# A two-step recurrence with its two normalisations apart, and its second set of weights at the other end of memory

## The chip, the cores and the metric

One core of a Trainium2 chip runs the whole program. The core has five engines, each with a queue of its own that it works through in order: TensorE (PE in the profile, its weight loads PEld), VectorE (DVE), ScalarE (ACT), GpSimd (POOL) and SyncE (SP), which here only starts DMAs. The metric is the device time of one execution in microseconds (us).

## The reference, cut to what matters

The input x has 2 sequences of 2048 tokens with 256 features, all float32. Six blocks add to it in turn, each on a layernorm of x:

```python
x = x + 0.5 * moe(layernorm(x))         # 6 experts, 2 per token, and a shared one
x = x + attention0(layernorm(x))        # 16 heads
x = x + 0.5 * moe(layernorm(x))         # the same weights
x = x + 0.5 * recurrence(layernorm(x))
x = x + attention1(layernorm(x))        # causal, rotary, relative positions
x = x + 0.5 * recurrence(layernorm(x))  # the same weights

def recurrence(x):      # the scan runs over the 2 sequences, so it has 2 steps
    c = in_c
    for xt in x:
        f = sigmoid(xt @ wf.T + c @ uf.T + bf)
        i = sigmoid(xt @ wi.T + c @ ui.T + bi)
        g = tanh(xt @ wc.T + c @ uc.T + bc)
        c = f * c + i * g
    return tanh(x @ wo.T + c @ uo.T + bo)
```

At the first step c is `in_c` for every token, so `in_c @ u.T + b` is a vector that is computed once.

## The kernel before, in words

x stays on the chip as 32 chunks of 128 tokens. Four chunks make a block of 512 tokens; blocks 0 to 3 are the first sequence (the recurrence's step 0), blocks 4 to 7 the second (step 1). Instructions are issued on each engine in the order in which the program is written; nothing reorders them.

A layernorm of a block is `stats` (L97 and L98 on VectorE for each chunk, then `root`, L102 and L104 on GpSimd), `normal` (L115, four instructions on VectorE, in some places on GpSimd), and `turn` (L125: eight TensorE transposes into two PSUM banks, copied out by ScalarE at L126). `Norm` keeps what is done in dictionaries, so that a block that was normalised or turned ahead is passed over. All PSUM use goes through eight banks, called `s`; normalised and turned blocks share eight slots, called `b`.

The mixture of experts works in two halves of 16 chunks. It scatters the tokens to memory sorted by expert, runs 74 tiles a half, and then adds the results back: `combine(h, c)` gathers two rows per token (L436, two indirect DMAs issued by GpSimd into a ring of ten `yg` tiles) and adds them with two L441 on VectorE. The second half's 16 combines can only come after the last expert tile; `rest(n)` issues the next n of them, followed by `last(c)`, which in the second mixture normalises a block of the next layer when its four chunks are complete. The shared expert's last two blocks (`up`, `mul`, `down`; evictions L349) run in the same place. Eight of the 16 combines stand there, and the other eight in the next layer.

The first attention is a list of jobs by step. In steps 0 to 8 only the largest scores are formed: a product (L756) and a reduction on VectorE (L760) for each of eight units a step, in two halves. Just ahead of step 0, GpSimd clears two small tiles (L556) and adds the output bias to four blocks (L588). In each half of steps 0 to 3, a combine of the rest follows the reductions. From step 9 the exponentials and weighted sums (L770, L775, L782) run beside them.

The recurrence holds the gates of a block as features by tokens. `gate(cb, step, m)` computes half m (128 features) of the three gates of block cb of a step: at step 0 six float32 products, at step 1 twelve, since the state is multiplied too (L146, two TensorE instructions to a product); then three activations on ScalarE (L896) and the new state on VectorE (L901 to L908). `first_bias` (L861 and L867) makes the three vectors of the first step; L861 is 24 small TensorE instructions. A loop over cb, four rounds, keeps step 0 a block ahead of step 1, and normalises and turns two blocks further on; `outputs` (L917 to L944) forms the result of a block pair one round late. In the first recurrence, `normals` and `turns` also normalise two blocks for the second attention in rounds 2 and 3, and the gates of step 0 are followed by `rest(2)`. In the second, blocks 0 and 4 are normalised and turned already in the tail of the second attention.

Memory is taken from pools that stack up from the left end or from the right end. A load into a place that earlier tiles held waits until those tiles have had their last reader. SP issues loads in order, so one that waits holds up those behind it. In the second recurrence the pool `wr` with the 13 weights (17 KB in each partition) lies at the right end, where the second attention's weights (`w1`, 9 KB) were; at the left end lay that attention's `mneg` tiles, its three `band` tiles and its values, and above them `part`, which collects the weighted sums. At the end of an attention group L658 transposes `part`, L672 its divided form, and L681 applies the output weights.

Of the kernel before, what the change touches and what calls it, by code (L numbers as in the profile page):

```python
# [27 lines left out]
CPB = TB // P  # L28
SB = S // TB
# [13 lines left out]
def macaron_kernel(ctx: ExitStack, tc: tile.TileContext, t: dict, out: bass.AP):  # L43
    nc = tc.nc
# [28 lines left out]
    def bank():  # L73
        return psum.tile([P, TB], F32, name="s")
# [7 lines left out]
    def pool(stack, name, bufs=1, side=None):  # L82
        return stack.enter_context(
            tc.tile_pool(name=name, bufs=bufs, side=side, reuse_waits="tile")
        )
# [72 lines left out]
    HB = NTB // 2  # L158
# [8 lines left out]
    def moe(w, ws, gate_w, gate_b, rev, tri, iota, z, behind, last, gathered):  # L167
# [3 lines left out]
        with ExitStack() as s:  # L171
# [333 lines left out]
            def rest(n):  # L505
                for _ in range(n):
                    c = next(chunks, None)
                    if c is not None:
                        combine(1, c)
                        last(c)  # L510
# [5 lines left out]
            down(6)  # L516
            rest(1)
            down(7)
            rest(4)
            if gathered is None:  # L520
                rest(HC)
            xnT.clear()
# [184 lines left out]
    def attention0(norm, tail, rest, wq, wk_, wv, wo, bff):  # L707
# [7 lines left out]
        with ExitStack() as s:  # L715
# [106 lines left out]
            for step in range(min(jobs), max(jobs) + 1):  # L822
                todo = jobs.get(step, [])
                for n in range(2):
                    z.begin(2 * step + n)
                    te, tm = (step - 9) // PER, step // PER
                    ke, um = ((step - 9) % PER) * 2 + n, (step % PER) * 2 + n
                    exps = 0 <= te < NG
                    last_j = 1 if exps else 3
                    for j in range(J):  # L830
                        if exps:
                            exponential(te, ke, j)
                        if 0 <= tm < NG:
                            largest(tm, um, (j + 2) % J if exps else j)
                    for fn, args in todo[n * (len(todo) + 1) // 2 :][: (len(todo) + 1 - n) // 2]:
                        fn(*args)
                    if step in range(4):
                        rest(1)
                    unit = 2 * (step - 9) + n - 1
                    if 0 <= unit < NG * NKB:  # L840
                        weighted(unit // NKB, unit % NKB)
# [3 lines left out]
    def recurrence(w, norm, store, rest, normals, turns):  # L845
# [3 lines left out]
        with ExitStack() as s:  # L849
# [18 lines left out]
                        bias0[n], pb[:, ds(2 * k, 2)], w[f"b{n}"], ALU.add  # L868
                    )

            def normal(cb):
                for step in range(2):
                    if step * SB + cb not in norm.xn:
                        norm.stats(step * SB + cb)
                        norm.normal(step * SB + cb, nc.vector)

            def turn(cb):
                for step in range(2):
                    if step * SB + cb not in norm.xnT:
                        norm.turn(step * SB + cb)  # L880
                    norm.xn.pop(step * SB + cb)

            def xnT(cb, step):
                return norm.xnT[step * SB + cb]
# [1 line left out]
            def gate(cb, step, m):  # L886

                g = {}
                for n, fn in GATES:
                    pg = bank()  # L890
                    mm2(pg, w[f"w{n}"], ts(m, P), xnT(cb, step), stop=step == 0)
                    if step == 1:
                        mm2(pg, w[f"u{n}"], ts(m, P), c1[cb], start=False)
                    bias = bias0[n] if step == 0 else w[f"b{n}"]
                    g[n] = wk.tile([P, TB], F32, name=f"g{n}")
                    nc.scalar.activation(g[n], pg, fn, bias=bias[:, m : m + 1])  # L896
                state = c1 if step == 0 else c2
                if m == 0:
                    state[cb] = wk.tile([P, 2, TB], F32, name=f"state{step}")
                c = state[cb][:, m, :]  # L900
                nc.vector.tensor_tensor(g["i"], g["i"], g["c"], ALU.mult)  # L901
                if step == 0:
                    nc.vector.scalar_tensor_tensor(
                        c, g["f"], w["in_c"][:, m : m + 1], g["i"], ALU.mult, ALU.add
                    )
                else:
                    nc.vector.tensor_tensor(c, g["f"], c1[cb][:, m, :], ALU.mult)
                    nc.vector.tensor_tensor(c, c, g["i"], ALU.add)  # L908
# [40 lines left out]
                    for half in range(CPB // 2):  # L949
                        output(cb, step, half, cu)  # L950

            normal(0)
            first_bias()
            turn(0)
            normal(1)
            for m in range(2):
                gate(0, 0, m)
                rest(2)
            turn(1)
            for cb in range(SB):  # L960
                if cb + 1 < SB:
                    for m in range(2):
                        gate(cb + 1, 0, m)
                        rest(2)
                if cb + 2 < SB:
                    normal(cb + 2)
                normals(cb)
                gate(cb, 1, 0)
                if cb + 2 < SB:
                    turn(cb + 2)  # L970
                turns(cb)
                gate(cb, 1, 1)
                if cb:
                    outputs(cb - 1)
            outputs(SB - 1)
# [436 lines left out]
    def recurrence_weights(wp):  # L1412
        return {
            n: load(wp, n)
            for n in (
                "wf", "uf", "wi", "ui", "wc", "uc", "wo", "uo", "bf", "bi", "bc", "bo", "in_c",
            )
        }

# [10 lines left out]
    with tc.manual_schedule(engines=ENGINES):  # L1430

        n0, n1, n2, n3, n4, n5 = (Norm() for _ in range(6))
        with ExitStack() as s:
            wp = pool(s, "wa0")


            ahead = Jobs()
            for b in range(SB):
                layernorm_jobs(ahead, n1, b, HC + 4 + CPB * b)

            weights = []

            def loads0():
                weights.extend(load(wp, n) for n in ("a0_q", "a0_k", "a0_v", "a0_o", "a0_b"))

            rest = run_moe(
                n0, ahead.run, nothing, loads0, clear=True, gathered=pool(s, "gathered")
            )
            tail = []
            for b in range(3):  # L1450
                tail += [(1 + 2 * b, n2.stats, b), (2 + 2 * b, n2.normal, b, nc.vector),
                         (3 + 2 * b, n2.turn, b)]
            tail.append((7, n2.stats, 3))
            attention0(n1, tail, rest, *weights)


        with ExitStack() as s:
            wr = pool(s, "wr")
            rec = {}

            def loads1():
                rec.update(recurrence_weights(wr))

            ahead = Jobs()
            for b in range(2):
                layernorm_jobs(ahead, n3, b, HC + 6 + CPB * b)

            def last(c):
                if c in (3, 7):
                    b = HB + c // CPB  # L1470
                    n3.stats(b)
                    n3.normal(b, nc.vector)

            rest = run_moe(n2, ahead.run, last, loads1, gathered=pool(s, "gathered"))
            w1 = ExitStack()
            wp = pool(w1, "w1", side="right")
            a = {n: load(wp, f"a1_{n}") for n in ("q", "k", "v", "o", "rel0_row")}
            relk, relv, rel0 = (load(wp, n) for n in ("relk", "relv", "rel0_col"))
            kbias = wp.tile([P, 2], F32, name="kbias")
            fp = pool(s, "rel")  # L1480
            relk0, relv0 = load(fp, "relk0"), load(fp, "relv0")

            def normals(cb):

                if cb == 1:


                    nc.vector.scalar_tensor_tensor(
                        kbias, rowsel[:, 0:2], rel0[:, 0:1], rowsel[:, 2:4], ALU.mult, ALU.add
                    )  # L1490
                    nc.vector.tensor_tensor(relk, relk, relk0, ALU.subtract)
                    nc.vector.tensor_tensor(relv, relv, relv0, ALU.subtract)
                if cb > 1:
                    n4.stats(cb - 2)
                    n4.normal(cb - 2, nc.vector)

            def turns(cb):
                if cb > 1:
                    n4.turn(cb - 2)
                    n4.xn.pop(cb - 2)  # L1500

            recurrence(rec, n3, False, rest, normals, turns)
        tail = []
        for i, b in enumerate((0, SB)):
            tail += [(3 + 2 * i, n5.stats, b), (4 + 2 * i, n5.normal, b, nc.vector),
                     (5 + 2 * i, n5.turn, b)]
        attention1(n4, tail, a, relk, relv, kbias, dramp, skew)
        w1.close()
        with ExitStack() as s:
            recurrence(recurrence_weights(pool(s, "wr", side="right")), n5, True, nothing, nothing, nothing)  # L1510


def _layout(i):
# [88 lines left out]
```

## Time and profile before

| | |
|---|---|
| three runs | 4068.05, 4071.13, 4072.09 us; median 4071.13 |
| the profiled execution | 4068.88 us, span in the profile 4067.0 us |
| granted TensorE clock, mean | 0.993 |
| first mixture, to the start of the first attention | about 0 to 347 us |
| first attention | to about 2050 us |
| second mixture | to about 2386 us |
| first recurrence | 2386 to 2578 us |
| second attention | to 3876 us |
| second recurrence | 3876 to 4067 us |

Times in the text are us from the start of the span. A row of the timeline gives the start, the duration, the engine, the line, the operation with what it writes and reads, and how many instructions it merges; in brackets stands how long the engine was idle before it, and what it waited for. A row of the waits gives who waited for whom, the sum in us, how often, and the longest. A row of the windows gives a stretch, its length, the busy time of PE, PEld, DVE, ACT and POOL (instructions in brackets), the clock that TensorE was granted as a share of full speed, the DMA engines' share, and GB/s.

### The profile page before, as it was taken

The numbers are of one execution on the slowest core, as the hardware profiler recorded it, in microseconds if no ns is written. First come the engines' busy times: TensorE is split into PE (matmuls) and PEld (weight loads), VectorE is DVE, ScalarE is ACT, GpSimd is POOL, SyncE is SP. The second block draws the span as 40 slices with busy tenths as digits, with TensorE's granted clock in tenths as the row PEclk, the third lists the DMA queues.
The fourth block names the chain that finished last, engine by engine and source line by source line (L and its number), as shares of the span: only waits on it lengthen the run. The fifth ranks groups of instructions, "written<-read, shape, count | busy, mean of one in ns | idle before, by whom it ended". The sixth has DMA issues, their size and how long they took to land.

```text
span 4067.0 us, 76436 instructions
## 1 busy us (share of the span) xinstructions
PE 3996.5 (98%) x28256; PEld 1930.7 (47%) x28256; DVE 2701.9 (66%) x6128; ACT 2568.8 (63%) x5227; POOL 1634.8 (40%) x1456
## 2 busy tenths in 40 slices
PE   8999999999999999999999999999999999999999
PEld 4665333333344333333356655555554455554445
DVE  6247888888866888888752444667677766677533
ACT  2333788888887888888833322366667766667832
POOL 4245333336333333333442340345635645544410
PEclk9999999999999999999999999999999999999999
DMA  7341000100000000000033420334533344442101
GB/s 256 122 128 58 1 1 1 48 1 1 1 1 1 1 1 1 1 1 1 10 110 126 129 76 0 78 82 104 111 71 74 82 81 87 91 96 49 45 22 42
DMA packets 355508, 223.18 MB, mean 55 GB/s; under 512 B 146624, under 2 KB 338496, under 8 KB 355136
## 3 DMA queue, kind: packets, MB, share of 16 engines
q1 hardware_dynamic: 276800, 176.33, 16.5%
q0 software_dynamic: 12288, 33.57, 2.6%
q10 hardware_dynamic: 66048, 8.39, 1.3%
q8 instruction: 225, 3.69, 0.4%
q14 instruction: 147, 1.20, 0.1%
HBM read 113.12 MB, written 105.12 MB: 54 GB/s over the span
## 4 chain that ended last, share of the span: by engine, by line
PE 90%; DVE 5%; POOL 1%; ACT 1%; issue 1%; DMA 0%; SPq 0%; POOLq 0%; ACTq 0%; DVEq 0%
PE s L770 13%; PE s L782 12%; PE s L756 10%; PE s L146 10%; PE s L1237 7%; PE s L1123 6%; PE s L383 6%; PE s L1208 6%; PE s L403 3%; PE s L681 2%; PE s L1222 1%; PE s L1201 1%; PE s L1218 1%; PE s L344 1%; PE s L931 1%
## 5 line engine op out<-in xcount | busy, mean ns | idle before, releaser
L542 POOL TENSOR_TENSOR part<-part 128x512 f32<-128x512 f32 (+3 forms) x800 | 962.0, 1203 | 1389.9 <-ACT part L644 1377.0
L760 DVE TENSOR_REDUCE mx<-s 128x1 f32<-128x512 f32 x2048 | 1271.0, 684 | 292.8 <-PE s L756 292.6
L775 ACT ACTIVATE pT<-s 128x512 f32<-128x512 f32 x2048 | 1063.6, 618 | 200.7 <-PE s L756 199.1
L756 PE MATMUL s<-kT,q 32*128 32x512 f32 x4096 | 1018.6, 618 | 1.9 <-DVE mx L760 1.9
L770 PE MATMUL s<-q,kT 32*128 32x512 f32 x4096 | 1013.0, 615 | 0.4 <-DVE q L639 0.4
L1229 ACT ACTIVATE pT<-s 128x512 f32<-128x512 f32 (+3 forms) x1280 | 587.8, 542 | 252.8 <-PE s L1208 102.0
L770 PEld LDWEIGHTS s<-q,kT 32*128 32x128 f32 x4096 | 417.8, 183 | 466.9 <-DVE mx L760 327.0
L644 ACT COPY part<-s 128x512 f32<-128x512 f32 (+3 forms) x864 | 508.2, 589 | 148.2 <-PE s L782 60.2
L1131 DVE TENSOR_REDUCE mx<-s 128x1 f32<-128x512 f32 (+1 forms) x768 | 473.0, 679 | 132.3 <-PE s L1123 123.9
L782 PE MATMUL s<-pT,v 128*32 128x512 f32 x4096 | 549.8, 605 | 0.6 <-ACT pT L775 0.2
L756 PEld LDWEIGHTS s<-kT,q 32*128 32x128 f32 x4096 | 406.4, 184 | 128.9 <-ACT pT L775 76.2
L1123 PE MATMUL s<-kT,q 32*128 32x512 f32 (+7 forms) x2240 | 332.1, 433 | 0.0
L1237 PE MATMUL s<-pT,v 128*32 128x512 f32 (+3 forms) x2560 | 304.7, 541 | 9.1 <-DVE mx L1131 5.0
L383 PE MATMUL s<-we,xT 128*128 x592 | 278.7, 593 | 0.2 <-ACT xT L378 0.2
L390 DVE TENSOR_TENSOR h<-sg,s 128x256 f32<-128x256 f32 x148 | 62.4, 422 | 289.5 <-ACT sg L388 289.3
L1123 PE MATMUL s<-b,q 32*128 32x512 f32 (+7 forms) x1280 | 243.0, 518 | 1.6 <-DVE v L612 1.4
L782 PEld LDWEIGHTS s<-pT,v 128*32 128x32 f32 x4096 | 82.1, 108 | 336.1 <-ACT pT L775 300.4
L1147 DVE CUSTOM_DVE_ANT_0 band<-s,band 128x160 f32<-128x160 f32 (+1 forms) x512 | 155.7, 314 | 127.2 <-PE s L1208 62.6
L542 POOL TENSOR_TENSOR band<-band,mneg 128x640 f32<-128x640 f32 x128 | 161.3, 1260 | 189.2 <-DVE mneg L1157 127.9
L1208 PE MATMUL s<-q,kT 32*128 32x512 f32 (+3 forms) x1152 | 236.3, 509 | 0.0
L436 POOL DMA_INDIRECT yg<-results,at x128 | 123.8, 967 | 235.0 <-DMA results<-y 197.6
L1208 PE MATMUL s<-q,b 32*128 32x512 f32 (+3 forms) x896 | 208.5, 568 | 0.0
(227 smaller groups left out, 5148.1 us busy)
## 6 DMA issues: line engine op xcount, KB each, us to landing
band<-skew SPq DMA_DIRECT2D x32, 1280.0 KB, 7.5
pd<-band SPq DMA_DIRECT2D x32, 1280.0 KB, 8.5
xs<-places SPq DMA_DIRECT2D x148, 128.0 KB, 2.2
results<-y SPq DMA_DIRECT2D x148, 128.0 KB, 1.7
places<-zero SPq DMA_DIRECT2D x2, 4736.0 KB, 16.4
we<-in_we SPq DMA_DIRECT2D x12, 768.0 KB, 11.6
skew<-s ACTq DMA_DIRECT2D x32, 256.0 KB, 3.0
s<-pd SPq DMA_DIRECT2D x32, 256.0 KB, 4.3
```

What stands on the lines that cost most here:

```text
L383: nc.tensor.matmul(pu, lhsT=xT[n][:, ts(kc, P)], rhs=w[:, kc, ds(val[n], 2 * D)], start=kc == 0, stop=kc == 1,)
L542: fn(*args)
L644: nc.scalar.copy(part[:, q0:], pv[:, q0:])
L756: nc.tensor.matmul(ps, lhsT=q[t][rows(j), ts(qb, P)], rhs=kT[b, g][rows(j), ts(kc, TB)], start=True, stop=True,)
L760: nc.vector.tensor_reduce(mx[t][:, qb * J + j, kc : kc + 1], ps, AX.X, ALU.max)
L770: nc.tensor.matmul(st, lhsT=kT[b, g][rows(j), ts(kb, P)], rhs=q[t][rows(j), :], start=True, stop=True,)
L775: nc.scalar.activation(z.pTs[t, kb, j], st, AF.Exp)
L782: nc.tensor.matmul(pv[rows(j), :], lhsT=v[b, g // 2][:, kb, ds(h * VW, 32)], rhs=z.pTs.pop((t, kb, j)), start=True, stop=True,)
L1123: nc.tensor.matmul(ps[:, ds(cols, n)], lhsT=lhsT, rhs=kT[b, c, g][rows(j), ds(k0, n)], start=True, stop=True,)
L1208: nc.tensor.matmul(ps[:, q0:], lhsT=k, rhs=q[t][rows(j), q0:], start=True, stop=True, skip_group_check=True,)
L1229: nc.scalar.activation(z.pTs[t, kb, j][:, q0:], st.pop((t, kb, j))[:, q0:], AF.Exp)
L1237: nc.tensor.matmul(pv[rows(j), q0:], lhsT=v[b, kb // CPB, g // 2][:, kb % CPB, ds(h * VW, 32)], rhs=z.pTs.pop((t, kb, j))[:, q0:], start=T ...
```

## The change

The combines that the mixture's own end issues become four instead of eight; in the first attention the others run in both halves of steps 0 to 5, and in the first recurrence behind six gates, two each. `last` normalises only the first block of the second half (block 4). In both recurrences `normal` and `turn` take one block at a time: step 1's blocks are normalised and turned one round later than step 0's blocks of the same number, and block 1's turn stands between the two gates of block 0. The 13 weights are loaded with the small vectors first, and the second recurrence's pool lies at the left end.

```diff
@@ end of moe
             down(7)
-            rest(4)
             if gathered is None:
                 rest(HC)
@@ attention0
-                    if step in range(4):
+                    if step in range(6):
                         rest(1)
@@ recurrence
-            def normal(cb):
-                for step in range(2):
-                    if step * SB + cb not in norm.xn:
-                        norm.stats(step * SB + cb)
-                        norm.normal(step * SB + cb, nc.vector)
-
-            def turn(cb):
-                for step in range(2):
-                    if step * SB + cb not in norm.xnT:
-                        norm.turn(step * SB + cb)
-                    norm.xn.pop(step * SB + cb)
+            def normal(cb, step):
+                if step * SB + cb not in norm.xn:
+                    norm.stats(step * SB + cb)
+                    norm.normal(step * SB + cb, nc.vector)
+
+            def turn(cb, step):
+                if step * SB + cb not in norm.xnT:
+                    norm.turn(step * SB + cb)
+                norm.xn.pop(step * SB + cb)
...
-            normal(0)
+            normal(0, 0)
             first_bias()
-            turn(0)
-            normal(1)
-            for m in range(2):
-                gate(0, 0, m)
-                rest(2)
-            turn(1)
+            turn(0, 0)
+            normal(1, 0)
+            gate(0, 0, 0)
+            rest(2)
+            turn(1, 0)
+            gate(0, 0, 1)
+            normal(0, 1)
+            rest(2)
             for cb in range(SB):
                 if cb + 1 < SB:
-                    for m in range(2):
-                        gate(cb + 1, 0, m)
-                        rest(2)
+                    gate(cb + 1, 0, 0)
+                    rest(2)
+                    if cb == 0:
+                        turn(0, 1)
+                    gate(cb + 1, 0, 1)
+                    rest(2)
                 if cb + 2 < SB:
-                    normal(cb + 2)
+                    normal(cb + 2, 0)
+                if cb + 1 < SB:
+                    normal(cb + 1, 1)
                 normals(cb)
                 gate(cb, 1, 0)
+                rest(2)
                 if cb + 2 < SB:
-                    turn(cb + 2)
+                    turn(cb + 2, 0)
+                if cb + 1 < SB:
+                    turn(cb + 1, 1)
                 turns(cb)
                 gate(cb, 1, 1)
+                rest(2)
                 if cb:
                     outputs(cb - 1)
@@ recurrence_weights
-                "wf", "uf", "wi", "ui", "wc", "uc", "wo", "uo", "bf", "bi", "bc", "bo", "in_c",
+                "bf", "bi", "bc", "in_c", "wf", "uf", "wi", "ui", "wc", "uc", "wo", "uo", "bo",
@@ second mixture
             def last(c):
-                if c in (3, 7):
-                    b = HB + c // CPB
-                    n3.stats(b)
-                    n3.normal(b, nc.vector)
+                if c == CPB - 1:
+                    n3.stats(HB)
+                    n3.normal(HB, nc.vector)
@@ second recurrence
-            recurrence(recurrence_weights(pool(s, "wr", side="right")), n5, True, nothing, nothing, nothing)
+            wr = pool(s, "wr")
+            recurrence(recurrence_weights(wr), n5, True, nothing, nothing, nothing)
```

## The prediction

> **What bounds the kernel now.** I read the engine shares and the chain of waits first, then the timelines of the three places that the change touches. TensorE carries the end; only holes in its row, and work that it does at half clock, can be won.
>
> ```profile
> PE 3996.5 (98%) x28256; PEld 1930.7 (47%) x28256; DVE 2701.9 (66%) x6128; ACT 2568.8 (63%) x5227; POOL 1634.8 (40%) x1456
> PE 90%; DVE 5%; POOL 1%; ACT 1%; issue 1%; DMA 0%; SPq 0%; POOLq 0%; ACTq 0%; DVEq 0%
> ```
>
> The first recurrence (2386 to 2578) has two holes, both before transposes of normalised blocks: 4.14 us for block 5, 3.35 us for block 6. After the first, ScalarE is late too.
>
> ```profile
> 2405.06 2.28 PE L125 MATMUL s<-ident,b 128*128 128x128 f32 x8 [4.14 <-DVE b L115]
> 2408.12 3.78 PE L146 MATMUL s<-b,wf 128*128 128x512 f32 x4 [0.78 <-ACT gf L896]
> 2436.29 2.21 PE L125 MATMUL s<-ident,b 128*128 128x128 f32 x8 [3.35 <-DVE b L115]
> ```
>
> The second recurrence begins with a wait for `in_c`, the last of 13 loads, of which the first had waited 41.2 us for L658, the last division's transposes (waits of SP, then the timeline):
>
> ```profile
> SPq L131 <- PE s L658: 41.2, 1, 41.2
> ```
>
> ```profile
> 3869.69 0.35 SPq L131 DMA_DIRECT2D wf<-in_wf  x1
> ...
> 3878.31 0.43 SPq L131 DMA_DIRECT2D in_c<-in_in_c  x1
> 3880.29 1.78 PEld L861 LDWEIGHTS s<-in_c,uf 128*128 128x128 f32 x8 [4.68 <-DMA bi<-in_bi]
> 3880.32 1.84 PE L861 MATMUL s<-in_c,uf 128*128 128x1 f32 x8 [4.31 <-DMA in_c<-in_in_c]
> ```
>
> The table of windows shows in its PEclk column (after the five busy times) what the hole leaves behind: half clock until about 3890.
>
> ```profile
> 3880.00:3886.00 6.00, 5.68 (x25) 5.62 (x26) 0.39 (x4) 0.15 (x1) 0.00 (x0) 0.51 0.01 3
> 3886.00:3890.00 4.00, 4.00 (x6) 1.51 (x5) 2.39 (x10) 1.81 (x2) 1.26 (x2) 0.50 0.00 0
> 3890.00:3894.00 4.00, 4.00 (x11) 1.75 (x10) 2.89 (x11) 1.37 (x2) 0.80 (x2) 0.96 0.00 0
> ```
>
> At the start of the first attention one combine instruction of VectorE (L441, median 485 ns) takes 9.97 us, while GpSimd does the bias additions:
>
> ```profile
> 350.82 9.97 DVE L441 SCALAR_TENSOR_TENSOR x<-yg,col,x 128x256 f32<-128x256 f32 x1
> 351.24 9.26 POOL L588 TENSOR_TENSOR x<-x,a_b 128x1024 f32<-128x1024 f32 x4
> 361.62 2.48 DVE L760 TENSOR_REDUCE mx<-s 128x1 f32<-128x512 f32 x4
> ```
>
> **The change, part by part.** No instruction or DMA is added or dropped: same gates, normalisations, transposes, gathers and loads, in another order. Units at full clock: a step-0 gate is 12 TensorE instructions, 5.15 us; a step-1 gate 24, 10.3; a turn (8 transposes) 0.86.
>
> *Four combines moved into the first attention.* Combine is two gathers on GpSimd (one per 1.25 us) and two L441 (0.92 us together). Before, VectorE reaches its first L760 at 361.62, though TensorE's first product (L756) is out at 356.34; it is VectorE-bound until about 408. Half a step is four L760 (2.39), with a combine 3.31. To the end of step 5 before: 361.62 + 8 x 3.31 + 0.3 + 4 x 2.4 = 398.0. After: it starts behind the product, at 356.7, with 12 combines: 356.7 + 12 x 3.31 = 396.4. Gain 1.6. GpSimd now meets memset and bias additions right behind the eight gathers of chunks 0 to 3, at 340.2; they end near 350.6, and chunk 4's gathers, with 2.9 us from issue to use, are there by 355, before their turn at 359.1. Here a rule speaks against the change. The Trainium skill, "SBUF — State Buffer", section "Who interferes with whom", says that a VectorE instruction with two SBUF inputs and a GpSimd instruction that reads SBUF exclude each other for whole instructions. The 9.97 us row agrees. So the additions, now at 341.1 to 350.6, would catch chunk 2's L441 (341.63 before), with four evictions (L349) behind it. By the rule VectorE resumes at 350.6 with four L441 and four L349, 4.8 us, and is done at 355.4: before 356.7, so the price is nothing. The four banks held can't stop TensorE, since four others are free for the projections that ScalarE empties. Without the rule the start is 356.7 as well. If the cover failed, the 4.8 us would cancel the gain: 1.6 us, between -3 and 2.
>
> *First recurrence.* Before, chunks 4 to 7 and block 5's normalisation stood on VectorE ahead of `first_bias`, so ScalarE got its biases at 2406. Now VectorE does the two evictions and the bias additions by 2391.3, and TensorE goes on from `first_bias` (ends 2388.95): three gates to 2404.4, block 4's turn (normalised at 2389.8) to 2405.3, a gate to 2410.45, the step-1 gate to 2420.75, block 2's turn to 2421.65. The next wait is block 5's. VectorE finishes the state of gate (1,0,1) 2.44 us after TensorE, 2412.9; two combines (2.0) to 2414.9; their gathers, the sixteenth at 2388.5 + 1.5 + 14 x 1.25 = 2407.5, have landed, because the two GpSimd roots now stand behind them. From the same rows of before (2427.04, 2435.73) block 5's normalisation starts 8.69 us later, 2423.55. The transposes start 0.56 behind it: the hole is 2.45 us, not 3.35. Queued on GpSimd behind block 5's root (2423.5) are the gathers of chunks 12 to 15; VectorE uses the last near 2441, and block 6 is first read for its statistics after gate (2,0,1), near 2450. That is cover.
> Is 2.45 us enough to lose the clock? The Trainium skill, "TensorE: Matmul & The Clock Gate", section "What's actually happening", puts both the idle and the busy window at about 3.4 us: no loss here. But the trace shows 0.50 in 3870 to 3872 after a hole of 2.18 us (and 0.29). I side with the row: 1.2 us, as after 2436 (the whole sum would be 22.3 by the rule, 21.1 by the row). The next gate's state product then starts at 2428.5, against 2440.70: 12.2 us won. Block 7's turn (0.86) still has to be done, now in round 2, and there it stands on VectorE ahead of the norm of the second attention, which ends 5.1 us later than its 2511.0. The turn ready at 2514.8 is held as in 2471.19 (loss 1.02 us by the starts of the next gate). Round 1 keeps its stall. Net 10.3; 8 to 13 with clock and gathers.
>
> *Second recurrence.* On the right the 17 KB of weights don't fit into the 9 KB that the attention's weights leave, so `wf` lies on `part`, which L658 reads at 3869. On the left they begin where the second attention's first tiles do: two `mneg` of 2 KB and bands of 10.4 KB, so they lie on `mneg` and the first two bands. Those are last read by the subtract transposes (3820) and the band transposes (L1218, last at 3843.2). The last older DMA of SP is issued at 3828.12; behind it all loads but `uo` and `bo` can start, and these two near 3843.5. Only the output stores (first at 3974.9) queue behind them. So 13 issues at 0.47 us and some 5 us of transfer leave the path. The new neighbour is `s<-pd`: it was issued first and takes 3.1 us, and its reader (L1254) runs at 3838.6, 7 us later. Its price is nothing; at most the 1.8 MB at the 362 GB/s seen in 3874 to 3876, 5 us, still inside that slack. `first_bias` then starts at 3876.0, not 3880.3: 4.3. At full clock it takes 2.6 us, as at 2386.35, not 5.1: 2.5; the first two gates 10.3 instead of 12.8: 2.5. By the clock page's 3.4 us window the half clock would have cost only about 1.7 us of these 5.0 and the gain would be 3.3 lower; the 0.50 rows last 9.8 us, and the trace decides. Block 1's turn now stands after one gate: its normalisation starts 3.7 us behind the bias additions, 3882.8, so the next gate starts at 3884.85 instead of 3884.67: loss 0.2. Gate (1,0,0) starts at 3889.95 against 3899.99: 10.0, less block 7's turn later (0.86, hidden on VectorE: ready 3 us ahead). Net 9.2, between 1 and 10.
>
> The new weight order costs nothing in the first recurrence: its loads run near 2052 to 2067, with first use at 2386.
>
> **Sum.** 1.6 + 10.3 + 9.2 = 21.1 us. The profiled run took 4068.9 (span 4067.0), 2.3 below the median of 4071.1; so 4047.8 for that run, and 4050.0 for the median.
>
> **Rivals.**
> Loads not early: some reader of the left region is later than I see, and the loads still end behind the last outputs. Small ones being first, about 1 us remains of part three: 21.1 - 8.2 = 12.9, 4058. Against it: nothing in the two `mneg` and two bands is read after 3844.
> The combines pace the first recurrence: with eight between gates, GpSimd's gather chain stays the path, as before (nearly all of 2388 to 2427). The hole ahead of block 5 then grows by up to 8 us: 4058. For it: L441 waited 0.7 us for each gather there. Against it: roots no longer split the chain.
> Slower: the 12 combines of the first attention run unprefetched, each waiting its gather's full 2.9 us in VectorE's queue ahead of the reductions, 35 us; then 4050 + 35 = 4085. It decides from 2.4 us a combine (29 us, the 21 plus 0.2%). Against it: ten `yg` buffers, and 0.3 us of such waits in that window.
>
> **Numbers.** My forecast 0.78 (4047 to 4057 by the bounds of parts one and two), loads late 0.08, gathers pace 0.08, both of these 0.03 (5 us left, 4066), slower 0.03. A measurement here can tell about 0.2%, 8 us, from no change. Faster: 0.78 + 0.08 + 0.08 = 0.94; same: 0.03. Range 4043 to 4060: it takes in the two milder rivals, and below 4047 the 4 us by which the runs shown differ.
>
> **What would show it.** Right: no wait of L861 for a DMA, clock 1.0 from 3876 on; `wf` issued near 3829; in the first recurrence no hole of 4 us near 2401 and one of 2 to 3 us ahead of block 5; L760 starting near 357. Wrong: a wait for `uo` or `in_c`, `s<-pd` landing after its reader is due, or VectorE idle for gathers between the reductions.

## The result, and the profile after

The kernel after takes 4050.03 us (median of 6 runs, 4046.7 to 4052.26), the kernel before 4069.84 (median of 6, 4067.27 to 4072.09): ratio 0.9954, 95% interval 0.9944 to 0.9964. The profiled execution took 4048.79 us, its span is 4046.9, and the granted clock was 0.995 on average (before: 0.993). The forecast was 4050.0. The lines of the changed kernel have other numbers than before by a few: L861 is L860, L760 is L759, L867 is L866, L658 is L657.

The engine shares in the page of the kernel after. TensorE is busy for 9.8 us less than before, though its instructions are the same ones: fewer of them ran at half clock, which makes 8.2 us by the clock records. The rest of the 20.1 us were holes.

```profile
PE 3986.7 (99%) x28256; PEld 1925.3 (48%) x28256; DVE 2698.4 (67%) x6128; ACT 2569.0 (63%) x5227; POOL 1634.6 (40%) x1456
```

The timeline of the first recurrence, kernel after (VectorE's bias additions, then TensorE). The biases are there at 2389.5 instead of 2406, the hole of 4.14 us is gone, and of the two holes one is left, 2.19 and 0.19 us ahead of block 5's transposes. Two rows are new: `wf` takes 3.01 us right behind the small products of L860, and 3.45 behind the hole, where such a row of four instructions takes 1.88 at full clock.

```profile
2389.34 0.14 DVE L866 TENSOR_TENSOR bias0f<-s,bf 128x2 f32<-128x2 f32 x1
2386.49 1.03 PE L860 MATMUL s<-in_c,uc 128*128 128x1 f32 x8
2387.39 3.01 PE L146 MATMUL s<-b,wf 128*128 128x512 f32 x4
2390.19 2.58 PE L146 MATMUL s<-b,wi 128*128 128x512 f32 x4
...
2424.17 0.56 PE L125 MATMUL s<-ident,b 128*128 128x128 f32 x2 [2.19 <-DVE b L115]
2424.93 1.24 PE L125 MATMUL s<-ident,b 128*128 128x128 f32 x6 [0.19 <-DVE b L115]
2425.97 3.45 PE L146 MATMUL s<-b,wf 128*128 128x512 f32 x4
```

The second recurrence, kernel after: SP's queue, TensorE, and then the table of windows (stretch, length, busy PE, PEld, DVE, ACT, POOL, clock, DMA share, GB/s). The loads are issued 47 us ahead of their use, L860 waits for nothing, and the clock is 1.00 where it was 0.51.

```profile
3818.11 1.19 SPq L131 DMA_DIRECT2D bf<-in_bf  x1
...
3833.18 0.43 SPq L131 DMA_DIRECT2D bo<-in_bo  x1
3865.18 0.95 PE L860 MATMUL s<-in_c,uf 128*128 128x1 f32 x8
3867.78 1.96 PE L146 MATMUL s<-b,wf 128*128 128x512 f32 x4
```

```profile
3864.00:3870.00 6.00, 6.00 (x36) 4.66 (x35) 2.98 (x12) 1.50 (x2) 0.00 (x0) 1.00 0.00 0
```

The start of the first attention, kernel after. GpSimd's additions come 10.4 us earlier than before and now catch a combine in the mixture's tail: of the two instructions in its row the first takes 8.85 us, to 0.3 us behind the end of the additions; the first reduction starts when TensorE's first product is there, 4.2 us earlier than before.

```profile
340.86 9.26 POOL L587 TENSOR_TENSOR x<-x,a_b 128x1024 f32<-128x1024 f32 x4
341.56 9.37 DVE L441 SCALAR_TENSOR_TENSOR x<-yg,col,x 128x256 f32<-128x256 f32 x2
357.43 0.69 DVE L759 TENSOR_REDUCE mx<-s 128x1 f32<-128x512 f32 x1 [3.18 <-PE s L755]
```

Where the time went, by stage. Each column is the difference of two starts in one profiled execution (us). "First attention's end" is the start of the last transposes of its divided outputs. The first recurrence runs from the first of the small bias products (L861, L860 after) to the last of its output products (L931, L928 after); the gap behind it ends at the first such transposes of the second attention. The last two columns count from the last start of the division's transposes (L658, L657 after): to the second recurrence's small products, and to the end. The last five kernels ran on two other chips (see the experiments).

| kernel | first attention's end | second mixture | first recurrence | gap behind it | small products behind division | end behind division |
|---|---|---|---|---|---|---|
| before | 2055.6 | 330.8 | 191.1 | 194.4 | 11.0 | 197.7 |
| after | 2055.7 | 329.1 | 183.1 | 193.2 | 6.6 | 188.3 |
| after, again | 2055.0 | 330.4 | 181.2 | 196.5 | 6.4 | 188.2 |
| old order, on the left | 2056.0 | 330.7 | 181.4 | 194.0 | 6.4 | 188.2 |
| first mixture's combines back | 2057.7 | 330.1 | 181.1 | 196.5 | 6.3 | 188.1 |
| turns late | 2055.4 | 329.1 | 176.2 | 196.8 | 6.3 | 186.0 |
| before, new order only | 2123.8 | 387.7 | 193.8 | 192.6 | 6.3 | 188.0 |
| before, split only | 2127.7 | 387.2 | 193.0 | 191.5 | 10.6 | 196.8 |
| after, combines back in both mixtures | 2124.5 | 387.4 | 193.1 | 194.4 | 6.4 | 188.1 |
| after, combines back in the second | 2121.3 | 388.2 | 193.2 | 194.4 | 6.4 | 188.2 |
| after, weights on the right | 2120.0 | 388.3 | 184.5 | 192.6 | 6.5 | 188.3 |

In the second mixture and in the gap TensorE's work is the same in all of these; among the first six rows the mixture differs by up to 1.7 us, and the gap by 3.6. That is the grain below which one profile of one kernel says nothing. The gain of the kernel after stands in the first recurrence and behind the division: 8.0 and 9.4 us in its first profile, 17.4 of the 20.1; the rest are differences of that grain. Of the 8.0, TensorE's idle time makes 5.9 (8.8 us before, 2.9 after) and time at half clock 1.7.

### The profile page after: what moved, and what is told of

It is laid out like the page before. It is cut to its first block, busy times and chain, and to the rows that moved or that the text cites. A ratio compares the mean times of both kernels' runs of the same rounds, so it can differ in the third digit from the quotient of the medians.

```text
span 4046.9 us, 76439 instructions
## 1 busy us (share of the span) xinstructions
PE 3986.7 (99%) x28256; PEld 1925.3 (48%) x28256; DVE 2698.4 (67%) x6128; ACT 2569.0 (63%) x5227; POOL 1634.6 (40%) x1456
## 4 chain that ended last, share of the span: by engine, by line
PE 90%; DVE 5%; POOL 2%; ACT 1%; issue 1%; DMA 1%; SPq 0%; DVEq 0%; ACTq 0%; POOLq 0%
PE s L769 13%; PE s L781 12%; PE s L755 10%; PE s L146 10%; PE s L1245 7%; PE s L383 6%; PE s L1131 6%; PE s L1216 6%; PE s L403 3%; PE s L680 2%; PE s L1230 1%; PE s L1209 1%; PE s L1226 1%; DVE mx L759 1%; PE s L928 1%; PE s L603 1%
## 5 line engine op out<-in xcount | busy, mean ns | idle before, releaser
L759 DVE TENSOR_REDUCE mx<-s 128x1 f32<-128x512 f32 x2048 | 1270.3, 682 | 297.6 <-PE s L755 297.1
```

The costliest lines, as they stand in the source:

```text
L759: nc.vector.tensor_reduce(mx[t][:, qb * J + j, kc : kc + 1], ps, AX.X, ALU.max)
```

## The experiments

The theory to begin with was the prediction's: the second recurrence gains because its weights lie where they can be loaded early; the first gains because the combines and block 5's layernorm left the way of the biases; the combines moved into the first attention gain little, as the profile after shows its end where it was. The rivals: the order of the loads does it, not their place; the combines in the first attention have a large share; the split of the layernorms has a gain of its own.

Eight of the twelve runs fell on two other chips, on which the kernel before takes 4196 us (medians 4196.36 and 4195.77), mostly because TensorE idles in the two mixtures there: the second takes 387 us instead of 331, with 45 us of idle TensorE instead of 3. The other four ran where before takes 4069.49, as in the comparison above (4069.84); in what follows that is the first chip. Each ratio is to runs of before on the same chip, and profiles are compared with profiles of the same group.

**The first part undone, with both mixtures touched.**

```diff
             down(7)
+            rest(4)
             if gathered is None:
...
-                    if step in range(6):
+                    if step in range(4):
```

> The kernel after, with the first part alone undone: the four combines stand in the first mixture again (rest(4) behind down(7), range(4) in the first attention). My theory by now: that part is worth nothing, because the 0.85 us by which VectorE is ahead in step 6 is eaten by a half-clock spell of TensorE that lasts longer; so the time of the kernel after, 4050, within 2 us, and the first product of the first attention that is read (the reduction of L759) at about 361.6 instead of 357.4. Rival, the prediction's sum: 1.6 us slower than after, 4051.6. Rival, the part was the whole gain: 4070.

Measured: 4188.3 us, ratio 0.998 (0.9972 to 0.9988), when the kernel with all of the change but the place of the weights has 0.9943 in the same group (below). That is far more than the few us expected, and the table says where: the first recurrence takes 193.1 us instead of 184. The edit was blunter than its text: the tail of the mixture is one function for both mixtures, and `rest(4)` came back in the second one too, ahead of the first recurrence. So the run is not a test of the first part; it showed how much hangs on the second mixture's four combines, with the reservation made below, where they come back alone.

**The weights alone, left and in the new order.**

```diff
-                "wf", "uf", "wi", "ui", "wc", "uc", "wo", "uo", "bf", "bi", "bc", "bo", "in_c",
+                "bf", "bi", "bc", "in_c", "wf", "uf", "wi", "ui", "wc", "uc", "wo", "uo", "bo",
...
-            recurrence(recurrence_weights(pool(s, "wr", side="right")), n5, True, nothing, nothing, nothing)
+            wr = pool(s, "wr")
+            recurrence(recurrence_weights(wr), n5, True, nothing, nothing, nothing)
```

> The kernel before, with the third part alone: the second recurrence's weights on the left of memory and in the new order. My theory: the loads end under the second attention, and the 4.3 us of wait and about 5 us of half clock go, less nothing (block 1's turn stands where it stood); 9 to 10 us faster than before, about 4060; the second recurrence from the last transposes of L658 on takes about 188 us instead of 198. Rival, the transfer was hidden anyway or a late reader of the left region still holds the loads: 0 to 1 us, 4069. If the clock after the hole had mattered only by the 3.4 us of the page, 6 us: 4064.

Measured: 4186.7 us, ratio 0.9977 (0.9968 to 0.9986), 9.7 us by the medians; the end comes 188.1 us behind the division's last transposes. This part stands by itself, and its size is as forecast.

**The split alone.** The kernel before with the changed recurrence and `last`; `rest(4)` stays at the end of both mixtures and `range(4)` in the first attention, the weights on the right in the old order.

```diff
-            normal(0)
+            normal(0, 0)
             first_bias()
-            turn(0)
-            normal(1)
+            turn(0, 0)
+            normal(1, 0)
...
-                if c in (3, 7):
+                if c == CPB - 1:
```

> The kernel before, with the second part alone: the recurrence's layernorms of the two parts apart and the combines behind six gates; the attention part undone, the weights of the second recurrence on the right and in the old order. My theory: 8 to 10 us faster than before, 4060 to 4062, all in the first recurrence (about 183 us from its first product of L861 to its end, instead of 191). In the second recurrence the split alone changes nothing that the late weights don't cover: about 198 us. Rival, the gather chain of the combines sets the pace there: 0 to 2 us, 4068.

Measured: 4198.12 us, ratio 1.0003 (0.9995 to 1.0011). The theory as written was wrong: on these chips the layernorms apart gain nothing while four more combines stand ahead of the biases (for the hole that takes their place, see "Four combines back in the second mixture"). The first recurrence takes 193.0 us, as with the code of before on the same chip (192.0 and 193.8 in the other two).

**The weights on the right again, only their order new.**

```diff
-            wr = pool(s, "wr")
+            wr = pool(s, "wr", side="right")
             recurrence(recurrence_weights(wr), n5, True, nothing, nothing, nothing)
```

> The kernel after, with the second recurrence's weights on the right of memory again and only their new order kept. My theory: the place is what counts, because the right side's free bytes end under the tiles that the last division's transposes read; so wf and uf wait for those again, the loads stand in the way, and the time goes back by 8 to 9 us to about 4058. The new order gives at most 1 us of it: the small loads land first but the u weights that the first products need still come late. Rival, the order alone does it (in_c no longer last): within 2 us of after, 4050 to 4052.

Measured: 4173.82 us, ratio 0.9943 (0.9929 to 0.9956). The theory fell. The end comes 188.3 us behind the division, as with the weights on the left, though the loads are as late as ever. Run once more later, beside the last group:

> The kernel after with the second recurrence's weights on the right of memory and in the new order, once more, beside the other parts. Theory: the place is worth nothing by itself, 0 to 2 us from after, 4048 to 4053. Rival, the place is worth the 8 us that the prediction gave to it: 4058.

Measured: 4171.93 us, ratio 0.9943 (0.993 to 0.9956).

**The order alone, in the kernel before.** The first two lines of the diff of the weights, and nothing else.

> The kernel before with one edit, the new order of the loads; the weights stay on the right of memory. Theory, from the run with the weights on the right: the order alone takes the wait away, since uc, the last load that the first products need, is then issued some 2.7 us behind wf and lands before they are due; 9 to 10 us faster than before, about 4060; the products of L861 6.3 to 6.6 us behind the last division's transposes (L658) instead of 11, and no half clock behind them. Rival, the prediction's own case of loads that are not early: 1 us faster, 4068.

Measured: 4187.43 us, ratio 0.998 (0.9971 to 0.9988), no different from the weights part whole. Its timeline, SP and then TensorE:

```profile
3995.80 0.33 SPq L131 DMA_DIRECT2D wf<-in_wf  x1
...
3998.07 0.43 SPq L131 DMA_DIRECT2D uc<-in_uc  x1
4001.98 0.33 SPq L131 DMA_DIRECT2D wo<-in_wo  x1
3995.08 0.65 PE L658 MATMUL s<-ident,part 128*128 128x128 f32 x4 [2.18 <-POOL part L542]
3997.45 4.49 PE L681 MATMUL s<-a_o,b 128*128 128x256 f32 x16
4001.78 0.95 PE L861 MATMUL s<-in_c,uf 128*128 128x1 f32 x8
```

`wf` is issued only behind the start of L658, just as before. But TensorE then still has 6.7 us of the attention's own work, and the six weights that the gates need are out 3 us after L658. What had held the first products before was a second wait in SP's queue, for the output products (L681): `uo` was issued 3.6 us after `wo`, and the small vectors stood behind it. Kernel before, two rows of SP's timeline and one of its waits:

```profile
3872.45 0.43 SPq L131 DMA_DIRECT2D wo<-in_wo  x1
3876.04 0.33 SPq L131 DMA_DIRECT2D uo<-in_uo  x1
```

```profile
SPq L131 <- PE s L681: 3.1, 1, 3.1
```

In the new order this wait falls on `wo`, 3.9 us after `uc`, and only `wo`, `uo` and `bo` stand behind it, which the outputs read much later.

**The old order on the left.**

```diff
-                "bf", "bi", "bc", "in_c", "wf", "uf", "wi", "ui", "wc", "uc", "wo", "uo", "bo",
+                "wf", "uf", "wi", "ui", "wc", "uc", "wo", "uo", "bf", "bi", "bc", "bo", "in_c",
```

> The kernel after, with the old order of the loads (wf first, in_c last) on the left of memory. The first theory, that the place is what counts, fell with the weights on the right in the new order: the loads were as late as before, but the first products did not wait. New theory: place and order each take the wait away by themselves, since only in_c and the three u weights hold the first products, and any of the two brings those in time; so within 2 us of the kernel after, the products of L860 6.5 us behind the last division's first transposes. Rival, the order alone matters: 8 to 9 us slower than after, the products 10.6 us behind.

Measured: 4049.55 us, ratio 0.9953 (0.9939 to 0.9966), beside 4051.86 for the kernel after. `in_c` is last again and waits behind `uo`, and is issued 30 us early all the same:

```profile
3819.42 1.16 SPq L131 DMA_DIRECT2D wf<-in_wf  x1
...
3833.86 0.33 SPq L131 DMA_DIRECT2D uo<-in_uo  x1
...
3836.13 0.43 SPq L131 DMA_DIRECT2D in_c<-in_in_c  x1
```

So place and order each take the whole wait away, and neither adds anything to the other.

**The kernel after, again.** No edit.

> The kernel after itself, unchanged, so that the parts measured beside it have the whole to stand against on the same chip. Both theories: 0.994 to 0.997 of before. Its trace also says how far a half-clock spell of TensorE differs from one profile to another at the same code: if such spells are fixed by the code, the one behind the products of L860 (0.57 of full clock in the 4 us after them) is there again; if they fall by chance it need not be.

Measured: 4051.86 us (4050.54 to 4053.85), ratio 0.9959 (0.9946 to 0.9973). In its profile the products behind L860 run at full speed, at the very place where they took 3.01 and 2.58 us in the first profile of the same kernel. The timeline of the second profile, and then the windows from 2388 to 2392 of the first and of the second:

```profile
2388.03 1.96 PE L146 MATMUL s<-b,wf 128*128 128x512 f32 x4
2389.83 1.88 PE L146 MATMUL s<-b,wi 128*128 128x512 f32 x4
```

```profile
2388.00:2392.00 4.00, 4.00 (x7) 1.63 (x6) 1.62 (x6) 1.97 (x2) 3.00 (x4) 0.57 0.34 98
```

```profile
2388.00:2392.00 4.00, 4.00 (x12) 1.85 (x12) 2.27 (x8) 1.78 (x2) 3.08 (x4) 1.00 0.22 66
```

In the five profiles on the first chip that have this order, the granted clock there was 0.57, 1.00, 1.00, 1.00 and 0.63. So it isn't fixed by the code; one such spell costs 1.7 to 2.0 us, the difference of 183.1 to the other three (181.1 to 181.4).

The clock records show what differs. In each of the 14 profiles all half-clock stretches start on one grid of 3.41 us steps, which lies elsewhere in each profile, and last one or more whole steps (the last one is cut off by the end). The kernel after, first profile, has one step at half clock there:

```profile
2388.20:2391.61 3.41, 3.41 (x5) 1.35 (x4) 1.42 (x6) 1.97 (x2) 2.55 (x3) 0.50 0.35 94
```

The products of L860 take 2.60 us. In the two profiles with the spell all of that lies in the one step ahead of it; in the three without, the grid cuts it, and no step holds more than 1.80, 2.08 and 1.86. Over both recurrences of all profiles, where the clock was full to begin with, half clock follows in 7 of 7 cases with 2.16 us or more of these products in one step, in 4 of 6 with 2.04 to 2.12, and in none of 13 with 1.93 or less. What looks like chance is the place of the grid.

**The first part undone, cleanly.** Four combines back in the first mixture alone, and `range(4)`.

```diff
             down(7)
+            if last.__name__ != "last":
+                rest(4)
...
-                    if step in range(6):
+                    if step in range(4):
```

> The kernel after, with four combines back in the first mixture alone (the second keeps its four out) and range(4) in the first attention: the first part undone and nothing else. Theory: that part is worth 0 to 2 us, so the time of after or up to 2 us more. Rival: the run with four combines back in both mixtures lost most of what the kernel after gains; if the first mixture has a share in this, 4 to 8 us slower than after; else all of it is the second mixture's, whose four combines stand ahead of the first recurrence.

Measured: 4049.68 us (4048.59 to 4054.66), ratio 0.9954 (0.9941 to 0.9968): on the first chip the first part is worth nothing that shows. The first reduction is back at 361.8, and the attention ends at 2057.7 in its one profile, behind 2055.0 to 2056.0 with the part and 2055.6 in the kernel before, which lacks it as well.

**Four combines back in the second mixture.**

```diff
             down(7)
+            if last.__name__ == "last":
+                rest(4)
```

> The kernel after with four combines back in the second mixture alone, so that they and the layernorm behind the fourth stand ahead of the first recurrence's biases on VectorE again; the layernorms stay apart. Theory: the first recurrence's gain lies in these four combines' being put off, and the layernorms apart are only what allows it: 8 to 10 us slower than after, 4059 to 4061, with an idle stretch of about 4 us ahead of the first gates. Rival: the split has a share of its own, block 5's turn is later but the rest stays: 2 to 5 us slower.

Measured: 4182.64 us, ratio 0.9969 (0.9958 to 0.9981), 9.5 us over the average of the two kernels of its group that have these four put off (4171.93 and the next one's 4174.39). The first recurrence takes 193.2 us, all of its gain gone (192.0 and 193.8 with the code of before). Its timeline, VectorE, ScalarE and TensorE:

```profile
2514.72 0.49 DVE L441 SCALAR_TENSOR_TENSOR x<-yg,col,x 128x256 f32<-128x256 f32 x1 [0.54 <-DMA yg<-results,at]
...
2524.03 0.15 DVE L868 TENSOR_TENSOR bias0f<-s,bf 128x2 f32<-128x2 f32 x1
2525.55 0.69 ACT L895 ACTIVATE gf<-s,bias0f 128x512 f32<-128x512 f32 x1
2537.91 0.69 ACT L895 ACTIVATE gc<-s,bias0c 128x512 f32<-128x512 f32 x1 [7.61 <-issue]
2545.55 1.07 ACT L126 COPY b<-s 128x512 f32<-128x512 f32 x2 [6.96 <-remote]
2546.19 3.78 PE L146 MATMUL s<-b,wf 128*128 128x512 f32 x4 [10.62 <-ACT b L126]
```

Eight combines, one per gather of 1.25 us, stand ahead of the biases, and ScalarE's first gate is at 2525.6 instead of 2514.8 (the weights on the right, second run). That was expected. What follows wasn't: no hole of 4 us, but one of 10.6. TensorE waits for a copy of ScalarE that comes late after two idle stretches, of 7.61 and 6.96 us, for which the trace names no engine ("issue", "remote"). The same hole, 10.5 to 10.6 us, stands in the other two runs that have the split and these combines ahead of the biases. Why ScalarE stops is not settled. Shorter stops of it, 2.5 us at the third gate of step 0, stand in the three runs on these chips that have the combines put off, and none there in the profiles of the first chip. So the run shows that the four combines, put off, carry the gain on these chips, but not by the theory's way: the late biases alone made no hole. Split and combines apart were not run on the first chip.

**The bias additions later.**

```diff
-                    at(-1, z.add_bias, qc)
+                    at(7, z.add_bias, qc)
```

> The kernel after with the first attention's four bias additions on GpSimd at its step 7 instead of ahead of it. Theory: the combine that took 9.37 us beside those additions takes about 0.5 us, VectorE is done some 8 us earlier with the mixture, and nothing comes of it, since the first product to be read comes from TensorE at 357 either way: first reduction at 357 to 358, the time within 2 us of after. Rival: the lock had a share in the end of the mixture; the first reduction 1 to 3 us earlier and as much off the time. Or the additions now catch two reductions in the attention, 8 us slower.

Measured: 4174.39 us, ratio 0.9951 (0.9938 to 0.9963), beside 0.9943 twice. The first reduction is at 414.7, with 413.5 to 415.6 in the three other profiles of these chips with the first part. VectorE is done with the mixture's tail early and waits 8.25 us instead of 3.18 for TensorE's first product. The additions catch a combine where they now stand (the first of the two instructions takes 9.31 us):

```profile
414.70 2.48 DVE L759 TENSOR_REDUCE mx<-s 128x1 f32<-128x512 f32 x4 [8.25 <-PE s L755]
440.03 9.24 POOL L587 TENSOR_TENSOR x<-x,a_b 128x1024 f32<-128x1024 f32 x4
440.26 9.83 DVE L441 SCALAR_TENSOR_TENSOR x<-yg,col,x 128x256 f32<-128x256 f32 x2
```

So the lock goes wherever the additions go, and in the mixture's tail its price is covered, as the prediction had it.

**A better version: the turns late.** In the kernel after, the holes that are left in both recurrences stand ahead of the second-step turns of the next block. Only the next round reads them.

```diff
                 gate(cb, 1, 0)
                 rest(2)
                 if cb + 2 < SB:
                     turn(cb + 2, 0)
+                gate(cb, 1, 1)
                 if cb + 1 < SB:
                     turn(cb + 1, 1)
                 turns(cb)
-                gate(cb, 1, 1)
                 rest(2)
```

> A version that should be better: the kernel after, with the second step's turn of the next block (and the turns of the second attention) moved from ahead of gate(cb, 1, 1) to behind it, since only the next round's second-step gate reads it. By the trace of after the transposes of block 5 waited 2.38 us and then ran a gate at half clock for 0.9 us, and the turns of rounds 1 and 2 of both recurrences held the next gate by 0.9 us each: 3.3 + 4 x 0.9 = 6.9. Theory: 5 to 7 us faster than after, with no idle time ahead of L125 in the first recurrence. Rival: the wait comes back at the next gate, because VectorE is behind there as well (its state and combines stand ahead of the evictions); 0 to 2 us.

Measured: 4041.29 us (4039.99 to 4042.86), ratio 0.9931 (0.9917 to 0.9944), beside 4051.86 for the kernel after in the same group; the kernels equal to after but for parts worth nothing had 4049.55 and 4049.68 there. So 8 to 11 us were won. In its timeline block 5's transposes follow the second half of the gate without a wait:

```profile
2420.68 1.04 PE L125 MATMUL s<-ident,b 128*128 128x128 f32 x8
2421.55 1.88 PE L146 MATMUL s<-b,wf 128*128 128x512 f32 x4
...
2431.86 1.04 PE L125 MATMUL s<-ident,b 128*128 128x128 f32 x8
```

The first recurrence takes 176.2 us, 6.9 less than 183.1 (both profiles have the spell behind L860), and the second 2.2 less: 9.1 in all, where 6.9 was expected. The excess is in the first recurrence, 6.9 for 3.3 + 1.8. By the starts of TensorE's instructions, its 64 transposes there take 12.3 us in the kernel after and 7.0 here: 5.3, of which the hole of 2.38 is a part. So the later turns gave 2.9 where 1.8 was expected, and the half clock behind the hole 1.6 where 0.9 was.

## Why the prediction was right or wrong

The time was right (4050.0 to 4050.03), the two large terms were right in size, and one small term and one cause were not. That the time was hit to 0.03 us is luck. The forecast took 21.1 us off a median of three runs, 4071.13; over six runs before has 4069.84, and the gain is 19.8. The two large terms gave 17.4 us in the profile for a forecast of 19.5, the third nothing for 1.6, and differences that nobody forecast made up the rest. The same kernel beside before once more was 17.6 us faster instead of 19.8.

- *Four combines into the first attention, 1.6.* Wrong in effect on the first chip: not told from nothing by time. The steps up to the first reduction held (forecast 356.7, measured 357.4; the additions at 341.1, measured 340.9; VectorE done at 355.4, measured 354.2). The failed term is the sum at the end of step 5: it treats VectorE as the bound to there and lets what it wins pass on to TensorE. Its lead of 4.2 us at the first reduction was down to 0.84 at the start of step 6, where 1.6 was forecast (it had started 0.7 later than forecast), and to 0.05 in the second half of step 9; the attention's end did not move. On the other chips the four profiles with the part end the attention at 2120.0 to 2122.9 and the four without at 2123.8 to 2129.1; there the first reduction is some 8 us earlier with it (413.5 to 415.6 for 421.1 to 424.9), not 4. That looks like a gain of a few us there. Two kernels differ in this part alone, the two with combines back, in both mixtures and in the second: 8.1 and 13.1 us faster than before, but each on its own chip and with overlapping intervals (0.9972 to 0.9988 and 0.9958 to 0.9981). So it stays open.
- *First recurrence, 10.3.* Right in size. Measured 8.0 in the first profile, 9.7 to 10.0 in the three without the spell behind L860 (191.1 less 181.1 to 181.4, beside one profile of before). The hole of 2.45 us ahead of block 5 was 2.38. Here the prediction weighed the Trainium skill, "TensorE: Matmul & The Clock Gate", section "What's actually happening", which would have taken no clock for so short a hole, against the row of 0.50 after 2.18 us of idle, and took 1.2 us of clock: the `wf` product behind the hole took 3.45 us for 1.88 in the first profile, 2.81 in the second, so the row was the better guide. What the sum lacked is that a spell can come without a hole. What the runs add to its reasoning: block 5's layernorm reads chunks 4 to 7, so while it stands ahead of the first gates, their combines can't be put off; the split frees them. That only putting them off gains is shown on the other two chips alone, where a stop of ScalarE fills the place of the hole; how the gain is shared on the first chip is open.
- *Second recurrence, 9.2.* Right in size: 9.4 to 9.6 by the table (11.0 less 6.3 to 6.6 for the wait, and 5.0 more for the half clock behind it, the two 2.5 of the forecast). Wrong in cause. The step that failed is the one behind the rival "loads not early": "Small ones being first, about 1 us remains of part three". The order alone gave the whole part, with the loads as late as before. The error was to follow the first load, which waits for L658, and not the last one that the first products need: before, `uo` was issued 3.6 us after the load ahead of it, and `in_c` stood 5 loads behind `uo`. That the weights can start 47 us earlier is true (`wf` went out at 3820.83, even before the 3829 of the forecast) and gains nothing more, and "the new weight order costs nothing" was said of the first recurrence alone, where it could gain nothing either.
- *Rivals.* The combines pacing the first recurrence: no, the first recurrence takes 181 us with two combines behind each of six gates, and the hole ahead of block 5 is 2.38 us and not some 10. The slower case, unprefetched combines in the first attention: no, its end is where it was.

## What to carry to other kernels

When a stage waits for a queue of loads, find the last load that its first instruction needs and what stands ahead of it in the queue; putting four small loads ahead was worth as much as starting all 13 loads 47 us earlier. A reordering can need a second one to pay: look for what the first one frees, and count the gain there. What feeds only the next round belongs behind this round's work, not ahead of it; and with half-clock spells that cost 2 us and come and go between runs of the same code, a single profile can't settle a term of that size.

## What the runs showed of the hardware

TensorE's half clock came and went on a grid of 3.41 us steps in every profile. Of the steps at full clock with 2 us or more of idle TensorE, 127 of 133 were followed by half clock; of those with less than 1 us idle, 38 of some 16,000. It also came with no idle time, behind the 2.6 us of products with one column each: in two of the five profiles of the first chip with the changed order, in all eight of the other two chips. GpSimd's four additions of 1024 elements held one VectorE instruction of a combine (0.49 us alone) for 9.97, 8.85 and 9.31 us where the two met, to 0.3 us behind the last of the four (9.26 us together) and not one at a time. On two other chips the same program was 3% slower, with TensorE idle in the mixtures. And ScalarE stood still for 7.6 and 7.0 us beside a run of gathers, for a reason that no row names.
